# A linear-attention stage: the place of the first units' bias additions, the engine of their copies, and one more unit in written-out order

## The chip, the cores and the metric

The kernel runs on one core of one Trainium2 chip. The metric is the device time of one execution in microseconds (us). A core has five engines with a queue each: TensorE (PE; its weight loads are listed as PEld), VectorE (DVE), ScalarE (ACT), GpSimd (POOL) and SyncE (SP), which issues transfers. Each queue is worked off in its order; engines wait for each other by semaphores.

## The reference

A small vision model: a tokenizer, then two layers, each an attention and a feed-forward block with a residual addition around each. The change lies in the attention of the second layer (the "linear attention"), which is computed so:

```python
def _L1_attn_ref(x, W_qkv, b_qkv, W_out, b_out):
    qkv = x @ W_qkv + b_qkv
    q, k, v = jnp.split(qkv, 3, axis=2)
    q = q - jnp.mean(q, axis=2, keepdims=True)
    k = k - jnp.mean(k, axis=2, keepdims=True)
    q2 = q * q
    k2 = k * k
    q2s = jnp.sum(q2, axis=2, keepdims=True)
    k2s = jnp.sum(k2, axis=2, keepdims=True)
    k2 = _l2_normalize(k2 / (k2s + EPS_DIV), axis=-2)
    q2 = _l2_normalize(q2 / (q2s + EPS_DIV), axis=-1)
    kv = jnp.einsum('bnc,bnd->bcd', k2, v)
    t2 = jnp.einsum('bnc,bcd->bnd', q2, kv) / math.sqrt(N)
    attn = v + t2
    return attn @ W_out + b_out
...
h = h + _L0_ffn_ref(_layernorm(h, axis=-1), ...)
h = h + _L1_attn_ref(_layernorm(h, axis=-1), ...)
h = h + _L1_ffn_ref(_layernorm(h, axis=-1), ...)
```

There are 4 images of 784 distinct rows with 256 columns (each stands three times in the output). `l2_normalize` over axis -2 makes k depend on all rows of an image; q is normalised row by row.

## The kernel before, in words

**Tiles and units.** Rows stand in tiles of 128: six full tiles an image, and one tile (the last) with the 16 rows left over of each image. `h` holds all 25 tiles on chip in f32. The linear attention works in units of three tiles: units 0 to 7 (two an image) and unit LU = 8, the tile of left-over rows.

**What a unit goes through.** `fetch` (GpSimd, L1643) gathers the two expert outputs of each row from memory into `ys`. `stats_one` (VectorE, L1657, L1674, L1675) adds them, weighted, to `h` (two L1657 per tile) and takes mean and variance. `norm_root` (ScalarE, L1687) and `norm_rows` (VectorE, L1696, L1699) make the normalised rows `xa`. `x_t` transposes `xa` on TensorE and copies the result from PSUM to `lxT`; `qk_mm` (TensorE, L1881), `qk_add` (VectorE, L1887) and `qk_squares` (ScalarE, L1895, L1896) make the squares of q and k with their sums; `root` (ScalarE), `factors` (VectorE, L1919 to L1923), `k_rows` (ScalarE, L1928), `q_rows` (VectorE, L1935), `k_squares` (ScalarE, L1942) and `fold` (VectorE, L1956 to L1961) make the normalised k (`uk`), q, and the sum of squares of an image. `q_t` transposes q into `lqT`.

**What an image goes through.** When both its units are ready: `k_x_tiles` multiplies `uk` with `xa` into `pukx` (TensorE, L1980), `k_x_left` adds the left-over rows (L1987), `k_norm` sums the folds over the rows (TensorE into `pn`, L1998 and L1999, then ScalarE L2004 and VectorE L2005), `k_x_out` scales into `g` (VectorE, L2012), `g_t` transposes `g` (TensorE L2028, ScalarE L2031), `kv_out` multiplies with the folded weight Wvo into `pkvo` and `kvo` (L2040, L2044). Then `rows_out(u)` computes, for each tile of a unit, x Wvo + q kvo into `pout` (TensorE, L2055 and L2060) and adds it to `h` (VectorE, L2066).

**Weights and the bias.** `layer1_weights` folds Wv and Wout into Wvo, and the biases into `bvo` and `bres` = bout + bvo (L734 to L753), in three steps taken by `next(steps)`. `residual(u)` (VectorE, L1714) adds `bres` to the three tiles of a unit in `h`. It has to come after the unit's `norm_rows`, which read `h` without it. Before, the first units that are normalised ahead of `bres` are put on the list `pending` and added at unit 3 (L2192); from there on each addition follows its `norm_rows`.

**Copies.** `copy_out` takes turns by a counter: odd to ScalarE (L89), even to VectorE (L91). `bias_relu` uses the same counter, every third to VectorE. The copies of unit LU's lxT go to VectorE without counting.

**What sets the order.** Units 0 to 2 stand in a block under `tc.manual_schedule`, in which the engines run in the order of the text (the scheduler may put instructions from outside the block between them, as it does with additions of L1714). From there on (the loop `for u in range(3, LU + 2)`, L2167) a scheduler sets the order from the dependencies and its own estimate of times. A manual dependency without a semaphore (`NoSync`) tells it only what must come after what on one engine. Seven PSUM buffers named `ps` go round. The last stage, the second feed-forward block with four experts (L2205 on), follows.

## Time and profile before

| | |
|---|---|
| median of 3 runs | 759.25 us (757.95 to 761.08) |
| profiled execution | 760.57 us, of which 758.9 us from the first to the last instruction (the span) |
| mean granted TensorE clock | 0.975 |
| VectorE busy over the span | 480.9 us (63%) |
| ScalarE busy over the span | 331.1 us (44%) |
| first product with Wqkv (unit 0) | 457.0 us |
| last gather issued | 518.0 us |
| loop of the last stage (L2209) | from 616 us to the end |

The profile is of one execution on the chip. Times in it count from the span's start. A group of instructions in order of time is given as start, length, engine, line, operation, tile written and tiles read, shapes and count; in brackets stands how long the engine was idle ahead of it and what ended that. "Clock" is the share of full speed that was granted to TensorE. A duration includes an instruction's start and end, so that independent instructions one behind the other follow at some 0.1 us less.

### The profile page before, as it was taken

How to read it: one execution, taken by the hardware profiler on the slowest of the kernel's cores; microseconds unless marked ns; L12 is line 12 of the kernel's file. 1: busy time of each engine (PE TensorE's matmuls, PEld its weight loads, DVE VectorE, ACT ScalarE, POOL GpSimd, SP SyncE). 2: the span in 40 equal slices, each digit the busy share in tenths (PEclk: the TensorE clock that was granted, in tenths of full speed). 3: DMA queues.
4: the chain of work that ended last, by engine and by line, in shares of the span. 5: the costliest groups of instructions: out<-in, count | busy, mean ns of one | idle time of the engine just before them, and what ended most of it. 6: DMA issues, size and time to landing. Idle time of an engine off the chain costs nothing.

```text
span 758.9 us, 10590 instructions
## 1 busy us (share of the span) xinstructions
PE 698.0 (92%) x3391; PEld 478.9 (63%) x3391; DVE 480.9 (63%) x1521; ACT 331.1 (44%) x782; POOL 127.1 (17%) x231
## 2 busy tenths in 40 slices
PE   6798989999996879998899999888999999999996
PEld 4645565666564568887788874557677765555553
DVE  4666786778999654456544767799957464444441
ACT  0554776555865554342222326353546322222231
POOL 5400000000034607600003036752000000000000
PEclk9999999999999879999999999899999999999998
DMA  8399999100011864422334352321000013222333
GB/s 196 89 426 424 425 424 424 48 1 1 0 36 48 275 239 136 157 83 78 91 98 125 98 161 71 88 79 43 1 0 2 4 29 114 93 76 62 125 108 98
DMA packets 56117, 96.24 MB, mean 127 GB/s; under 512 B 6375, under 2 KB 46030, under 8 KB 56062
## 3 DMA queue, kind: packets, MB, share of 16 engines
q1 hardware_dynamic: 49648, 79.38, 29.6%
q0 software_dynamic: 5536, 14.32, 6.2%
q10 hardware_dynamic: 878, 1.86, 1.0%
q8 instruction: 27, 0.44, 0.2%
q14 instruction: 28, 0.23, 0.1%
HBM read 30.45 MB, written 65.09 MB: 126 GB/s over the span
## 4 chain that ended last, share of the span: by engine, by line
PE 69%; DVE 19%; ACT 5%; DMA 3%; issue 2%; SPq 1%; DVEq 1%; ACTq 0%
PE pb L1420 12%; PE pe L289 6%; PE pyb L1438 5%; PE ps L289 4%; PE pqk L1881 4%; PE pkv L289 4%; PE pt L280 4%; PE pw L558 3%; PE pwp L300 3%; PE ps L2256 3%; PE pout L2055 3%; PE pout L2060 3%; DVE oT L868 2%; PE pukx L1980 2%; DMA img<-in_x_dram 2%
## 5 line engine op out<-in xcount | busy, mean ns | idle before, releaser
L1059 POOL DMA_INDIRECT xrows<-xn,pos x50 | 52.6, 1051 | 238.0 <-DVE nm L918 191.9
L1643 POOL DMA_INDIRECT ys<-yrows,pos x50 | 51.7, 1033 | 142.7 <-DMA yrows<-yb 124.3
L1420 PE MATMUL pb<-xTb,own 128*128 128x256 f32 (+1 forms) x240 | 54.5, 371 | 8.1 <-DVE own L1396 5.4
L1426 ACT ACTIVATE hb<-pb,own 128x256 f32<-128x256 f32 (+1 forms) x74 | 33.8, 456 | 57.8 <-PE pb L1420 51.5
L1420 PE MATMUL pb<-hb,own 128*128 128x256 f32 (+1 forms) x240 | 52.1, 359 | 0.6 <-DVE hb L1428 0.6
L1438 PE MATMUL pyb<-own,hb 128*128 128x256 f32 x216 | 51.8, 381 | 0.2 <-ACT hb L1426 0.2
L1420 PEld LDWEIGHTS pb<-xTb,own 128*128 128x128 f32 x240 | 41.7, 195 | 16.1 <-ACT hb L1426 7.6
L1881 PE MATMUL pqk<-Wqkv,lxT 128*128 128x512 f32 x100 | 46.6, 613 | 0.2 <-ACT lxT L89 0.2
L289 PE MATMUL pe<-xT,eW 128*128 128x512 f32 (+1 forms) x112 | 46.0, 553 | 0.0
L1438 PEld LDWEIGHTS pyb<-own,hb 128*128 128x128 f32 x216 | 40.3, 190 | 5.9 <-ACT hb L1426 0.6
L1420 PEld LDWEIGHTS pb<-hb,own 128*128 128x128 f32 x240 | 40.5, 190 | 5.3 <-DVE hb L1428 1.2
L558 PE MATMUL pw<-Wall,pT 128*128 128x512 f32 x96 | 42.6, 593 | 0.0
L1409 ACT COPY xTb<-ptb 128x512 f32<-128x512 f32 (+1 forms) x30 | 16.2, 540 | 56.4 <-PE ptb L1405 56.4
L1444 DVE TENSOR_TENSOR yb<-pyb,eb 128x512 f32<-128x512 f32 (+1 forms) x30 | 19.1, 638 | 33.9 <-PE pyb L1438 33.5
L280 PE MATMUL pt<-ident,xn 128*128 128x128 f32 x200 | 30.4, 282 | 10.2 <-DVE xn L584 6.6
L280 PEld LDWEIGHTS pt<-ident,xn 128*128 128x128 f32 x200 | 23.5, 142 | 25.2 <-ACT y L561 6.0
L1428 DVE TENSOR_SCALAR hb<-pb,own 128x256 f32<-128x256 f32 (+1 forms) x46 | 20.5, 447 | 27.9 <-PE pb L1420 21.2
L822 DVE SCALAR_TENSOR_TENSOR prod<-kq 128x784 f32<-128x784 f32 x32 | 30.4, 970 | 6.1 <-ACT kq L1236 3.4
L289 PEld LDWEIGHTS pe<-xT,eW 128*128 128x128 f32 x112 | 20.2, 190 | 21.6 <-issue 16.5
L1396 DVE COPY own<-ew 128x1540 f32 x30 | 28.9, 965 | 6.8 <-ACT xTb L1409 2.7
L1895 ACT ACTIVATE qk<-qk 128x256 f32<-128x256 f32 x50 | 20.4, 408 | 28.4 <-DVE qk L1887 26.0
L1881 PEld LDWEIGHTS pqk<-Wqkv,lxT 128*128 128x128 f32 x100 | 19.0, 197 | 20.4 <-issue 17.9
(416 smaller groups left out, 1473.4 us busy)
## 6 DMA issues: line engine op xcount, KB each, us to landing
xrows<-nothing SPq DMA_DIRECT2D x22, 896.0 KB
yrows<-nothing SPq DMA_DIRECT2D x22, 896.0 KB
out_dram<-h SPq DMA_DIRECT2D x23, 384.0 KB
xb<-xrows SPq DMA_DIRECT2D x24, 256.0 KB
yrows<-yb SPq DMA_DIRECT2D x24, 256.0 KB
ew<-in_L_ffn_expert_w_dram SPq DMA_DIRECT2D x6, 768.0 KB
wb<-wd SPq DMA_DIRECT2D x16, 128.0 KB
img<-in_x_dram SPq DMA_DIRECT2D x2, 588.0 KB
```

Source lines behind the costliest of these rows:

```text
L280: nc.tensor.transpose(pt[:, j * TT : (j + 1) * TT], xn[:, j, c * P : (c + 1) * P], ident[:TT, :TT])
L289: nc.tensor.matmul(pm[: wcols.stop - wcols.start, :n], w[:, c, wcols], xT(c), start=(c == 0), stop=(c == chunks - 1),)
L300: nc.tensor.matmul(pm[:, i, :], xT(c, t), w[:, c, :], start=(c == 0), stop=(c == chunks - 1))
L558: nc.tensor.matmul(pm, pixels(c, tiles[j]), Wall[:, c, :], start=(c == 0), stop=(c == 1))
L822: nc.vector.scalar_tensor_tensor(prod, qTs[s][:, o, :], 1.0, kT[:, o, t * SEQ : (t + 1) * SEQ], ALU.mult, ALU.mult, accum_out=atts[s][:, o ...
L1059: put = nc.gpsimd.indirect_dma_start(out=xrows[:, :], out_offset=bass.IndirectOffsetOnAxis(ap=pos[:, k, t0 + j : t0 + j + 1], axis=0), in_ ...
L1396: nc.vector.tensor_copy(w, ewf[0][:, bass.ds(off, EW)])
L1420: nc.tensor.matmul(pm, wm[:, c, o * P : (o + 1) * P], src[:, c, :], start=(c == 0), stop=(c == 1),)
L1426: nc.scalar.activation(dst[:, o, :], pm, AF.Relu, bias=b)
L1438: nc.tensor.matmul(pm[:, t, :], src[:, c, t * P : (t + 1) * P], wm[:, c, :], start=(c == 0), stop=(c == 1),)
L1643: got = nc.gpsimd.indirect_dma_start(out=y[:, j, k, :], out_offset=None, in_=yrows[:, :], in_offset=bass.IndirectOffsetOnAxis(ap=pos[:, k, ...
L1881: nc.tensor.matmul(pqk, xTs[u][:, c, cut(j, 1)], Wqkv[:, c, : 2 * D], start=(c == 0), stop=(c == 1),)
```

## The change

1. A switch `one_side` is on for the written-out block: every `copy_out` in it goes to ScalarE. The copies for `bvs`, `WvT` and `bvo` and those of unit LU's lxT go to ScalarE as well; unit LU's now count in the turn.
2. `residual` is held for the first seven units that are normalised (0, 1, LU, 2, 3, 4, 5). They are added after `rows_out` of units 3 (in the loop at u = 5: units 0 and 1), 4 (u = 6: LU and 2) and 5 (u = 7: 3, 4 and 5), each with an order-only dependency on the last addition of that `rows_out`. Units 6 and 7 are added behind their `norm_rows` as before.
3. In the written-out block, unit 2's statistics and rows move forward, ahead of unit LU's factors and the first folds.
4. The written-out block goes on for one more unit: unit 3, the statistics and rows of unit 4, its transposes and `rows_out` of unit 1 (now a generator, so that its two parts can be placed apart). The loop begins at 4. Statistics of units 5 and later (`behind`) may come no earlier than the end of `rows_out(1)`; before, those of units 4 and later no earlier than the end of `rows_out(0)`.

```diff
@@ copy_out
+    one_side = [False]
...
-        if turn[0] % 2:
+        if one_side[0] or turn[0] % 2:
             nc.scalar.copy(dst, src)
         else:
             nc.vector.tensor_copy(dst, src)
@@ layer1_weights
         for k in range(2):
-            nc.vector.tensor_copy(bvs[:, k, :], col("bv", k).to_broadcast([P, P]))
-        nc.vector.tensor_copy(WvT, pt)
+            nc.scalar.copy(bvs[:, k, :], col("bv", k).to_broadcast([P, P]))
+        nc.scalar.copy(WvT, pt)
...
-        nc.vector.tensor_copy(bvo, pw)
+        nc.scalar.copy(bvo, pw)
@@ norm_rows, residual
-        if pending is None:
+        if len(pending) < 7:
+            pending.append(u)
+        else:
             residual(u)
-        else:
-            pending.append(u)
...
-    def residual(u):
+    def residual(u, last=None):
...
-        nc.vector.tensor_tensor(ht, ht, over(lw[2], n), ALU.add)
+        added = nc.vector.tensor_tensor(ht, ht, over(lw[2], n), ALU.add)
+        if last:
+            tc.add_manual_dep(
+                added.ins, last,
+                mybir.DependencyInfo(mybir.DependencyClass.NoSync, mybir.DependencyReason.DATA),
+                reason="where VectorE has time",
+            )
@@ x_t
-        copy = nc.vector.tensor_copy if u == LU else copy_out
-        transposed(xa_of(u), n, lambda c, pt: copy(xT[:, c, : n * TT], pt))
+        transposed(xa_of(u), n, lambda c, pt: copy_out(xT[:, c, : n * TT], pt))
@@ rows_out
     def rows_out(u):
+        for done in rows_out_parts(u):
+            pass
+        return done
+
+    def rows_out_parts(u):
...
-            done = nc.vector.tensor_tensor(ht, pm[:, : len(two), :], ht, ALU.add)
-        return done
+            yield nc.vector.tensor_tensor(ht, pm[:, : len(two), :], ht, ALU.add)
@@ the written-out block
+    one_side[0] = True
     with tc.manual_schedule(engines=by_hand | {ENG.Pool}):
...
         q_rows(0)
+        stats_one(2, 0)
         next(steps)
         x_t(LU)
         q_t(0)
         k_rows(0)
         next(steps)
-        stats_one(2, 0)
+        stats_one(2, 1)
         factors(1)
         q_rows(1)
         k_rows(1)
         qk_mm(LU, 0)
+        stats_one(2, 2)
+        norm_root(2)
         next(steps)
         Wvo, bvo = lw[:2]
         q_t(1)
         qk_add(LU, 0)
         qk_squares(LU, 0)
         root(LU)
-        stats_one(2, 1)
-        stats_one(2, 2)
+        norm_rows(2)
         fetch(5)
-        norm_root(2)
         squares[0] = k_squares(0)
         factors(LU)
         fold(0, squares.pop(0))
-        norm_rows(2)
         k_rows(LU)
...
-        behind.append(rows_out(0).ins.name)
+        rows_out(0)
         x_t(3)
-    squares[2] = scales(2)
-    fold(2, squares.pop(2))
-    for u in range(3, LU + 2):
+        root(2)
+        factors(2)
+        k_rows(2)
+        q_rows(2)
+        fetch(6)
+        for j in range(2):
+            qk_mm(3, j)
+            qk_add(3, j)
+            qk_squares(3, j)
+            stats_one(4, j)
+        squares[2] = k_squares(2)
+        qk_mm(3, 2)
+        qk_add(3, 2)
+        qk_squares(3, 2)
+        stats_one(4, 2)
+        root(3)
+        norm_root(4)
+        norm_rows(4)
+        parts_ = rows_out_parts(1)
+        next(parts_)
+        fold(2, squares.pop(2))
+        factors(3)
+        k_rows(3)
+        q_t(2)
+        x_t(4)
+        for done in parts_:
+            pass
+        q_rows(3)
+        squares[3] = k_squares(3)
+        fold(3, squares.pop(3))
+        behind.append(done.ins.name)
+    one_side[0] = False
+    later = {5: (0, 1), 6: (2, 3), 7: (4, 5, 6)}
+    for u in range(4, LU + 2):
...
-        if u == 3:
-            for k in pending:
-                residual(k)
-            pending = None
-        rows_out(u - 2)
+        done = rows_out(u - 2)
+        for k in later.get(u, ()):
+            residual(pending[k], done.ins.name)
```

`later` holds places in the list `pending`, whose order is 0, 1, LU, 2, 3, 4, 5.

## The prediction

> **What bounds the kernel now.** Read in this order: the page's first part, the chain of waits, the engines in order of time through the first units of the linear attention, and the granted clock in 2 us windows. Page, part one:
>
> ```profile
> PE 698.0 (92%) x3391; PEld 478.9 (63%) x3391; DVE 480.9 (63%) x1521; ACT 331.1 (44%) x782; POOL 127.1 (17%) x231
> ```
>
> TensorE is busy for 92% of the span. A new order can only win in the other 8% and in stretches at a lower clock. The chain of waits from 519 us to the end (start, length, what):
>
> ```profile
> 531.15 3.44 PE pqk L1881 x8
> ...
> 601.41 0.59 ACT gT L2031
> ```
>
> From 519.84 us the chain is TensorE almost throughout, with one break of 0.6 us at 601.4 (a ScalarE copy) until the last additions at 752. 531.15 is the start of unit 4's product with Wqkv; from there 221 us of TensorE work follow without a gap worth naming. What moves this start moves the end by as much, if VectorE and ScalarE keep up. Before it the chain runs over VectorE. TensorE in order of time, with the idle time ahead of each group and its releaser in brackets:
>
> ```profile
> 470.86 1.99 PE L741 MATMUL pwvo<-Wout,WvT 128*128 128x256 f32 x8 [0.54 <-DVE WvT L735]
> ...
> 484.06 1.30 PE L280 MATMUL pt<-ident,xa 128*128 128x128 f32 x6 [2.64 <-DVE xa L1699]
> ...
> 505.37 5.48 PE L1881 MATMUL pqk<-Wqkv,lxT 128*128 128x512 f32 x12 [0.24 <-ACT lxT L89]
> 514.77 1.22 PE L280 MATMUL pt<-ident,xa 128*128 128x128 f32 x6 [3.93 <-DVE xa L1699]
> ```
>
> With 0.83 at 497.30 (pkvo, for ScalarE's gT) these are all its waits from 470 to 545. The two large ones are for `xa`, the normalised rows of units 2 and 4 (L1699). The windows (length, then busy us of PE, PEld, DVE, ACT and POOL, the granted clock, the DMA share and GB/s):
>
> ```profile
> 482.00:484.00 2.00, 0.00 (x0) 0.00 (x0) 1.41 (x6) 1.97 (x7) 1.39 (x2) 1.00 0.28 74
> ...
> 486.00:488.00 2.00, 2.00 (x8) 1.30 (x6) 1.35 (x4) 0.00 (x0) 1.70 (x2) 0.50 0.05 10
> ...
> 512.00:514.00 2.00, 0.00 (x0) 0.00 (x0) 2.00 (x9) 1.68 (x8) 1.41 (x2) 1.00 0.23 66
> ...
> 516.00:518.00 2.00, 2.00 (x6) 1.57 (x6) 2.00 (x6) 2.00 (x7) 1.39 (x3) 0.50 0.36 119
> ```
>
> After each large wait TensorE runs at clock 0.50. By 0.2 us windows the half clock lasts from 485.3 to 492.1 and from 516.0 to 519.4: 6.8 and 3.4 us. In these TensorE has no idle time, so the loss is half: 3.4 + 1.7 = 5.1 us. Why VectorE is late with unit 2's rows is seen in its own order of time:
>
> ```profile
> 469.67 0.61 DVE L734 COPY bvs<-cols 128x128 f32<-128x128 f32 x1
> 470.13 0.68 DVE L735 COPY WvT<-pwv 128x512 f32<-128x512 f32 x1
> ...
> 477.73 0.95 DVE L1714 TENSOR_TENSOR h<-h,bout 128x768 f32<-128x768 f32 x1
> ...
> 483.59 1.06 DVE L1699 TENSOR_SCALAR xa<-h,mv,rstd 128x256 f32<-128x256 f32 x3
> ```
>
> Between the q rows of unit 0 (end 469.6) and unit 2's `xa` stand copies (bvs, WvT, two for unit LU, two lqT, bvo), bias additions (L1714: 0.95, and 0.42 at 479.00) and unit LU's factors with a fold that waits for ScalarE. For unit 4 the chain of waits shows:
>
> ```profile
> 513.44 0.86 DVE h L1657 x2
> 514.30 0.34 DVE xa L1699
> ```
>
> Two L1657 that belong to unit 5 are pulled ahead of unit 4's rows; a bias addition (0.84 at 510.73) stands before them.
>
> [...] (6.8 and 3.4 us are two windows and one; the two onsets lie 30.7 us apart, nine windows) [...] waits of 2.64 and 3.93 us sufficed, with TensorE busy in about 1.2 us of the window before the fall. [...] here the two L1657 at 471.59 took 1.56 us beside GpSimd's L2104 (470.25 to 473.95) and 0.99 elsewhere, so +0.57. [...] the trace has 0.48 and 0.55 (L89, L91), so the moved copies get no dearer.
>
> **The change, part by part.** The program's order is known for every engine: up to the q rows of unit 0 only one copy (second half of unit 1's lxT) differs; GpSimd's and SP's orders don't differ at all, so all gathers stand where they stood.
>
> (a) Copies to ScalarE. Up to unit 2's rows VectorE loses bvs and WvT and the lxT of LU and lqT of unit 0 (469.61 to 471.67: 2.06 us) and bvo and one lqT (0.43 + 0.46). ScalarE gets them in its queue: after root(1) at 470.4 come two bvs (not shown on ScalarE; between 0.24, its 128-column copy, and 0.37, its 256-column one; less 0.1 of overlap each: about 0.4 for both, ends 0.3 to 0.55) and WvT (0.58 as gT L2031), so WvT is ready at 471.35 and not 470.75. TensorE's wait of 0.54 grows by 0.55. Nothing hides that: cost 0.55.
>
> (b) Bias additions. L1714 of units 0, LU, 2 and later are gone from 477.7 on; seven are held and put after rows_out of units 3, 4 and 5. VectorE in order, from 469.61: statistics of unit 2, three times 1.6 us (two L1657, L1674, L1675), two of them +0.57; factors(1) 0.72; q rows 0.91: at 477.2. Then it waits for ScalarE (rstd 0.3, bvo 0.37) and does bout (0.42), the qk addition of LU (0.60), reciprocal and three `xa` rows (0.35 each): rows ready from 479.5 to 480.2, not from 484.0. The gathers they need were issued at latest at 469.28, land in 2.7 us, and are asked for at 475.6: hidden.
>
> (c) TensorE from 471.35: pwvo 1.72, pqk of LU 1.72, pbvo 0.87, lqT 0.66, pukx 5.35: 481.7 to 482.0. Unit 2's transposes find their rows. Their lxT copies, both on ScalarE now, stand behind all k squares. ScalarE: squares of LU from 478.9, root, k squares of unit 0 to 481.4, LU's row, then four squares (483.1), two lxT copies (484.0). TensorE is at its pn at 483.6 and asks for lxT at 484.25: met by 0.25 us, so a delay above that comes through. The wait of 2.64 and the cold 6.8 us go. The next wait, for gT (0.83), stays, since it hangs on the same three ScalarE squares. pkvo starts at 490.9 where the trace has 497.30: 6.4 us gained (2.64 + 3.4 + 0.6 of row-by-row waiting in the transposes, less 0.55, and 0.3 of pipeline ends).
>
> (d) Order carried on. pkvo 1.73, pout of unit 0 5.17, transposes 0.65, wait 0.3, so unit 3's pqk at 498.8 to 503.9; two tiles of pout of unit 1 (3.45) and lqT of unit 2 (0.66) now stand ahead of unit 4's transposes: 508.05. VectorE meanwhile: factors(2) at 500.0 (root(2) stands behind two lxT copies on ScalarE), q rows 0.9, then three times a qk addition (0.60) and statistics of unit 4 (1.6): 507.5; rstd 0.3, reciprocal, rows from 508.5 to 509.2. TensorE waits some 0.65 in all, where it waited 3.93 and then had 3.4 us cold. Last tile of pout 1.72, pukx, pn and the left part 6.9, lqT of unit 3 0.66: unit 4's pqk at 518.6, not 531.15. That is 6.1 more (3.3 of wait, 1.7 of cold clock, 0.6 row by row, 0.5 pipeline ends), 12.5 so far.
>
> What ScalarE queues here: k rows of unit 3 wait for factors(3) at about 511, and lqT of unit 2 and lxT of unit 4 stand behind them, ready at 514. TensorE asks for lxT(4) at 518.6: hidden, 4 us to spare. The fold's last addition is at about 516, as pn comes up: 0 to 0.5.
>
> (e) Later units. The late bias additions, 0.87 each, are on VectorE's queue: two of them stand ahead of the last fold addition of unit 5, for which pn of image 2 waits: between 0 (fold done in time) and 1.7; I take 1.0. The added dependency only orders, it brings no semaphore wait. The other five stand beside gate and softmax work, under TensorE's 5 us pqk groups. VectorE's load bears it: from 470 to 620 it is busy 113.6 us, of which some 6.3 us are copies now on ScalarE; 107 us remain for about 138. In the last stage ReLUs change engine (unit LU's copies now count in the turn: both of e1 go to ScalarE, s2 and one s1 to VectorE), each needed 2 us or more after it is ready: 0, or up to 0.2 in each of seven groups, 1.4 in all.
>
> Sum: 12.5 - 1.0 = 11.5 us. The profiled execution took 760.57 (span 758.9), so 749.1; its own span would be 747.4. It lies 1.32 above the median of 759.25, about what one cold window more or less is worth (1.7), and so the gain against the median is 10.2.
>
> **Rivals.**
> 1. Smaller gain, a new cold window. TensorE waits at 470.3 for 1.05 us, after 1 us of small waits since 467.9; by the trace a window with 1.2 us busy fell, one with 1.76 (509.1 to 512.5) did not. Here some 1.1 to 1.3 are busy in the window that would end at 471.65. For: that. [...] Cost 1.7 to 3.4; with 0.5 for thin lxT margins and 0.4 more at the end, 752 to 754, say 753.
> 2. Off the path but given back: VectorE has fewer statistics done ahead (the trace has the last L1657 of all units at 536.2), so units 5 to 7 meet them inside TensorE's time. If each of the two rows of units 5 and 6, two pn and two g waits costs 1.2, 7.2 are lost: 756.3, no change. Against: VectorE needs about 14.0 of TensorE's 16.2 us per unit (qk additions 1.8, factors 0.5, q rows 0.9, fold 1.05, rows_out 0.95, copies 0.95, half an image's kn, g and kvo 1.0, statistics 4.8, rows 1.15, bias 0.9).
> 3. Slower. The one mechanism: VectorE falls behind in units 4 to 7, because its strict queue holds held additions ahead of folds and g; TensorE then waits at pn of images 1 to 3, and each wait over 2.6 us brings a half clock of 3.4 us more. Three waits of 3.5 plus three times 1.7 is 15.6: 764.7. It decides only if VectorE's 14.0 us per unit become 21. Against: from 498 to 546 VectorE was busy nearly throughout, and after 520 TensorE didn't wait.
> 4. The change doesn't do what it says: excluded by the order, in which the additions do stand late.
>
> **How the numbers follow.** Forecast 0.73, rival 1 0.17, rival 2 0.06, rival 3 0.04. The forecast's own range is 746.5 to 751.5 (no loss in (e) to 1.7 + 1.4, and 1 us of scatter); with most of rival 1 the range is 746 to 753.5. What a measurement can tell here is about 0.5%, 3.8 us: faster is below 755.45. Forecast and rival 1 are faster, rival 2 the same, rival 3 slower: 0.90, 0.06, 0.04.
>
> **What would show it.** Right: no TensorE wait above 1.2 us between 470 and 530 and clock 1.00 there; pkvo at about 491, unit 4's pqk at about 518.6; no L1714 ahead of that pqk (the trace of before has six by 516). Wrong: clock 0.50 after 471.65 (rival 1); waits for VectorE at pn L1998 or pkvo after 520 (rivals 2 and 3); a wait for lxT from ScalarE near 484 would show that the moved copies became the bound. If the two cold stretches were the accident of this one execution, the gain against the median shrinks by up to 3 us.

## The result, and the profile after

| | kernel before | changed kernel |
|---|---|---|
| median of the runs | 760.16 us (757.95 to 762.25) | 750.86 us (750.06 to 751.87) |
| profiled execution: time | 760.57 us | 750.06 us |
| profiled execution: span, granted clock | 758.9 us, 0.975 | 748.2 us, 0.982 |

The ratio after to before is 0.9876, with a 95% interval of 0.9848 to 0.9905: 9.3 us of the medians and 10.5 us between the two profiled executions. The first part of the changed kernel's page:

```profile
PE 692.6 (93%) x3391; PEld 476.9 (64%) x3391; DVE 475.4 (64%) x1506; ACT 333.1 (45%) x795; POOL 125.4 (17%) x231
```

TensorE's busy time is 5.4 us less (698.0 before) for the same 3391 products. That is for the most part half clock that is gone (5.1 us by the prediction's count). The rest of the 10.7 us of span is idle time that is gone. Which waits they were is seen in TensorE's order of time (start, length, line, operation, and in brackets the idle time ahead and its releaser), the same view that the prediction shows of the kernel before:

```profile
471.37 1.99 PE L742 MATMUL pwvo<-Wout,WvT 128*128 128x256 f32 x8 [1.00 <-ACT WvT L736]
...
481.65 0.82 PE L281 MATMUL pt<-ident,xa 128*128 128x128 f32 x6
...
483.64 0.38 PE L2004 MATMUL pn<-ones,acc 128*128 128x1 f32 x2 [0.29 <-DVE acc L1967]
...
491.70 1.99 PE L2046 MATMUL pkvo<-Wvo,gT 128*128 128x256 f32 x8 [1.10 <-ACT gT L2037]
...
499.77 5.42 PE L1887 MATMUL pqk<-Wqkv,lxT 128*128 128x512 f32 x12 [0.24 <-ACT lxT L90]
...
509.55 1.21 PE L281 MATMUL pt<-ident,xa 128*128 128x128 f32 x6 [0.25 <-DVE xa L1700]
```

Of the two large waits for `xa`, the one of 2.64 us is gone (481.65 carries no bracket) and the one of 3.93 us has become 0.25. Two other waits have grown: for WvT from 0.54 to 1.00 and for gT from 0.83 to 1.10. A small one is new, 0.29 for the fold at pn. The windows (busy us of PE, PEld, DVE, ACT and POOL, granted clock, DMA share, GB/s):

```profile
482.00:484.00 2.00, 1.71 (x13) 1.25 (x11) 1.27 (x4) 1.42 (x5) 1.50 (x2) 1.00 0.25 66
486.00:488.00 2.00, 2.00 (x6) 0.83 (x5) 1.97 (x5) 0.62 (x3) 1.54 (x2) 1.00 0.37 98
512.00:514.00 2.00, 2.00 (x11) 1.76 (x10) 1.48 (x5) 2.00 (x6) 1.70 (x2) 1.00 0.46 131
516.00:518.00 2.00, 2.00 (x14) 1.67 (x13) 1.90 (x7) 0.00 (x0) 0.00 (x0) 1.00 0.22 66
```

At 486 and 516 us the clock column reads 1.00 where it read 0.50; no stretch between 446 and 548 us is at half clock. VectorE in order of time shows why the rows are early:

```profile
469.57 1.09 DVE L1658 SCALAR_TENSOR_TENSOR h<-ys,wk,h 128x256 f32<-128x256 f32 x2
...
471.26 1.25 DVE L1658 SCALAR_TENSOR_TENSOR h<-ys,wk,h 128x256 f32<-128x256 f32 x2
...
477.30 0.42 DVE L754 TENSOR_TENSOR bout<-bout,bvo 128x256 f32<-128x256 f32 x1 [0.62 <-ACT bvo L752]
477.64 0.68 DVE L1893 TENSOR_TENSOR qk<-pqk,bqkv 128x512 f32<-128x512 f32 x1
...
478.44 1.06 DVE L1700 TENSOR_SCALAR xa<-h,mv,rstd 128x256 f32<-128x256 f32 x3
...
508.99 1.06 DVE L1700 TENSOR_SCALAR xa<-h,mv,rstd 128x256 f32<-128x256 f32 x3
...
531.40 0.95 DVE L1715 TENSOR_TENSOR h<-h,bout 128x768 f32<-128x768 f32 x1
```

The rows of unit 2 (L1700, 478.44) come behind bout's addition and one qk addition, 5.2 us earlier than before. No bias addition (L1715) stands ahead of them or of unit 4's rows at 508.99; the first is at 531.40. The chain of waits of the changed kernel from 518.9 us on (start, length, what):

```profile
518.91 0.65 PE pukx L1993 x3
519.56 0.66 PE pt L281 x6
520.22 3.44 PE pqk L1887 x8
```

Unit 4's product starts at 520.22, where it was 531.15: 10.93 us gained, of which 10.67 remain at the end of the chain. The later units gave back about 0.3.

### The profile page after: what moved, and what is told of

It reads as the page before. It is cut to its first block, busy times and chain, and to the rows that moved or that the text cites. A ratio compares the mean times of both kernels' runs of the same rounds, so it can differ in the third digit from the quotient of the medians.

```text
span 748.2 us, 10591 instructions
## 1 busy us (share of the span) xinstructions
PE 692.6 (93%) x3391; PEld 476.9 (64%) x3391; DVE 475.4 (64%) x1506; ACT 333.1 (45%) x795; POOL 125.4 (17%) x231
## 4 chain that ended last, share of the span: by engine, by line
PE 69%; DVE 18%; ACT 7%; DMA 2%; issue 2%; DVEq 1%; ACTq 0%
PE pb L1421 12%; PE pe L290 6%; PE pyb L1439 5%; PE ps L290 4%; PE pqk L1887 4%; PE pkv L290 4%; PE pt L281 3%; PE pw L559 3%; PE ps L2296 3%; PE pwp L301 3%; PE pout L2066 3%; PE pout L2071 3%; DMA img<-in_x_dram 2%; DVE oT L869 2%; PE pukx L1986 2%
## 5 line engine op out<-in xcount | busy, mean ns | idle before, releaser
L1644 POOL DMA_INDIRECT ys<-yrows,pos x50 | 49.2, 983 | 141.2 <-DMA yrows<-yb 124.4
L1887 PE MATMUL pqk<-Wqkv,lxT 128*128 128x512 f32 x100 | 44.9, 594 | 0.2 <-ACT lxT L90 0.2
L1439 PEld LDWEIGHTS pyb<-own,hb 128*128 128x128 f32 x216 | 40.3, 190 | 5.8 <-ACT hb L1427 0.6
L281 PE MATMUL pt<-ident,xn 128*128 128x128 f32 x200 | 29.9, 278 | 10.7 <-DVE xn L585 6.6
L559 PEld LDWEIGHTS pw<-Wall,pT 128*128 128x128 f32 x96 | 18.0, 190 | 19.9 <-issue 17.7
L1887 PEld LDWEIGHTS pqk<-Wqkv,lxT 128*128 128x128 f32 x100 | 18.4, 190 | 19.3 <-issue 17.0
```

What stands on the lines that cost most here:

```text
L281: nc.tensor.transpose(pt[:, j * TT : (j + 1) * TT], xn[:, j, c * P : (c + 1) * P], ident[:TT, :TT])
L559: nc.tensor.matmul(pm, pixels(c, tiles[j]), Wall[:, c, :], start=(c == 0), stop=(c == 1))
L1439: nc.tensor.matmul(pm[:, t, :], src[:, c, t * P : (t + 1) * P], wm[:, c, :], start=(c == 0), stop=(c == 1),)
L1644: got = nc.gpsimd.indirect_dma_start(out=y[:, j, k, :], out_offset=None, in_=yrows[:, :], in_offset=bass.IndirectOffsetOnAxis(ap=pos[:, k, ...
L1887: nc.tensor.matmul(pqk, xTs[u][:, c, cut(j, 1)], Wqkv[:, c, : 2 * D], start=(c == 0), stop=(c == 1),)
```

## The experiments

The ratios stand against runs of the kernel before on the same chip. Executions also differ by up to 3 us in the first 457 us, which no kernel here changes (the first product with Wqkv, unit 0's, starts between 456.5 and 459.4 in the fourteen profiles; the recorded expectations call it unit 1's). So each profile is also read from that product on, and the time column is used to see whether the reading holds. The columns: median of the runs and ratio with interval; then, from unit 0's product, the us to pkvo of image 0 and to unit 4's product; from unit 0's product to the last output transfer that ScalarE issues; and the half clock between 460 and 540 us, in us.

| kernel | median | ratio | pkvo | unit 4 | end | half clock |
|---|---|---|---|---|---|---|
| before | 760.16 | | 40.3 | 74.0 | 295.9 | 10.2 |
| changed | 750.86 | 0.9876 [0.9848, 0.9905] | 34.7 | 63.0 | 285.2 | 0 |
| bias_early | 752.09 | 0.9892 [0.9873, 0.9911] | 35.7 | 64.5 | 286.7 | 3.4 |
| copies_back | 752.72 | 0.9900 [0.9883, 0.9916] | 38.0 | 66.4 | 288.6 | 6.8 |
| block_short | 751.72 | 0.9887 [0.9869, 0.9906] | 34.7 | 64.1 | 286.0 | 0 |
| bias_alone | 755.67 | 0.9947 [0.9930, 0.9964] | 36.3 | 69.1 | 291.0 | 3.4 |
| stats_back | 753.14 | 0.9915 [0.9896, 0.9934] | 36.6 | 64.9 | 287.0 | 0 |
| bias_inblock | 752.72 | 0.9909 [0.9890, 0.9928] | 36.6 | 65.8 | 287.7 | 3.4 |
| warm | 758.80 | 0.9981 [0.9970, 0.9993] | 37.7 | 71.3 | 293.1 | 3.4 |
| copies_stats | 759.59 | 1.0001 [0.9987, 1.0015] | 36.2 | 70.4 | 293.2 | 10.2 |
| after_again | 749.57 | 0.9872 [0.9847, 0.9898] | 34.7 | 63.1 | 285.2 | 0 |
| after_warm | 751.26 | 0.9896 [0.9870, 0.9921] | 34.9 | 63.2 | 285.4 | 0 |
| better | 750.13 | 0.9880 [0.9860, 0.9899] | 33.4 | 61.7 | 283.8 | 0 |
| better_again | 750.24 | 0.9885 [0.9859, 0.9911] | 33.6 | 61.8 | 284.0 | 0 |

The starts are those of TensorE in order of time, where unit 4's product of the changed kernel stands at 520.05. From unit 4's product to the end all fourteen take 221.8 to 222.8 us: everything is decided between 457 and 531 us.

Each profile is of one execution. Two profiles of the same kernel agree to 0.2 us in these columns (changed and after_again, better and better_again). The times are coarser: by their intervals bias_early, copies_back, block_short, stats_back and bias_inblock can't be told from the changed kernel, and only bias_alone, warm and copies_stats stand clear of it. What the five are said to cost is read from their profiles.

**bias_early: the additions let go as before, all at the loop's first turn (now u = 4), the rest of the change kept.**

```diff
-        if len(pending) < 7:
-            pending.append(u)
-        else:
+        if pending is None:
             residual(u)
...
-        done = rows_out(u - 2)
-        for k in later.get(u, ()):
-            residual(pending[k], done.ins.name)
+        if u == 4:
+            for k in pending:
+                residual(k)
+            pending = None
+        rows_out(u - 2)
```

> The changed kernel with its bias additions of the first units back where the kernel before let them go: all held ones together after rows_out of unit 2's turn (u == 4), later ones right behind the rows of their own unit; no order tie. Copies on ScalarE, unit 2's statistics early and the order carried on through unit 4's rows stay. Theory A (the time came from getting unit 2's and unit 4's rows out earlier, by whatever means, and the hold list already keeps the additions behind unit 4's rows here, because the release now comes after the written-out block): unit 4's pqk (L1887) still starts at 520 +-1 us, time about 750.5, within 1 us of the changed kernel. Theory B (the later placement of the additions is what brings the gain; the order around them only follows): three to five additions of 0.87 us stand in VectorE's way again, folds and gates of units 2 to 5 come late, waits of TensorE return after 520 us: 754 to 758.

Measured: 752.09, ratio 0.9892; unit 4's product 64.5 us after unit 0's, where the changed kernel needs 63.0. VectorE in order of time, additions (L1715) and rows (L1700) of units 2 to 4:

```profile
479.55 0.40 DVE L1715 TENSOR_TENSOR h<-h,bout 128x256 f32<-128x256 f32 x1
479.87 1.05 DVE L1700 TENSOR_SCALAR xa<-h,mv,rstd 128x256 f32<-128x256 f32 x3
...
480.96 0.96 DVE L1715 TENSOR_TENSOR h<-h,bout 128x768 f32<-128x768 f32 x1
...
499.45 0.95 DVE L1715 TENSOR_TENSOR h<-h,bout 128x768 f32<-128x768 f32 x1
...
500.86 0.96 DVE L1715 TENSOR_TENSOR h<-h,bout 128x768 f32<-128x768 f32 x1
...
510.47 1.06 DVE L1700 TENSOR_SCALAR xa<-h,mv,rstd 128x256 f32<-128x256 f32 x3
```

The additions are back among the rows: 0.40 us stand ahead of unit 2's, and 1.9 us (499.45, 500.86) ahead of unit 4's. Yet the wait for unit 4's rows is 0.24 us. Most of the 1.5 us have another source, which TensorE and the windows of this kernel show:

```profile
471.82 3.26 PE L742 MATMUL pwvo<-Wout,WvT 128*128 128x256 f32 x8 [1.00 <-ACT WvT L736]
```

```profile
472.00:474.00 2.00, 2.00 (x6) 1.59 (x7) 1.90 (x5) 2.00 (x7) 2.00 (x3) 0.60 0.00 0
474.00:476.00 2.00, 2.00 (x5) 1.23 (x4) 1.78 (x8) 1.21 (x5) 1.79 (x2) 0.55 0.00 0
```

Behind the same wait of 1.00 us that the changed kernel has, 3.4 us at half clock follow here: pkvo comes 1.0 us later. Half of 3.4 would be 1.7; 0.3 of the wait at pn and 0.1 of that for gT were taken up, and 0.3 stays unexplained. The other 0.5 us arise between pkvo and unit 4's product. So theory A in the main, with a half clock on top, but not as it was put: it had the additions behind unit 4's rows, and they stand ahead of them. By this profile the late additions are worth some 0.5 us when the rest of the change is in place. And the prediction's first rival, a half clock after the wait for WvT, is real; the profiled execution of the changed kernel was spared it.

**copies_back: bvs, WvT, bvo and unit LU's lxT copied by VectorE again, and the switch `one_side` off,** so that the other copies of the written-out block take turns as before.

```diff
-            nc.scalar.copy(bvs[:, k, :], col("bv", k).to_broadcast([P, P]))
-        nc.scalar.copy(WvT, pt)
+            nc.vector.tensor_copy(bvs[:, k, :], col("bv", k).to_broadcast([P, P]))
+        nc.vector.tensor_copy(WvT, pt)
...
-        nc.scalar.copy(bvo, pw)
+        nc.vector.tensor_copy(bvo, pw)
...
-        transposed(xa_of(u), n, lambda c, pt: copy_out(xT[:, c, : n * TT], pt))
+        copy = nc.vector.tensor_copy if u == LU else copy_out
+        transposed(xa_of(u), n, lambda c, pt: copy(xT[:, c, : n * TT], pt))
...
-    one_side[0] = True
```

> The changed kernel with the copies of bvs, WvT, bvo and unit LU's lxT on VectorE again (as in the kernel before) and nothing else undone. Theory A (the copies are 2 to 3 us of VectorE's work just ahead of unit 2's rows, part of its lateness there): VectorE now does three statistics of unit 2 ahead of them or between, WvT is late, TensorE waits 2 to 2.5 us at pwvo instead of 1.0, and some 1.8 us are lost: 752.5; if this wait brings the half clock on, 1.7 to 3.4 more, 754 to 756. Theory B (the copies were hidden anyway, only the additions mattered): 750.5 +-0.7, wait at pwvo not above 1.2.

Measured: 752.72. The wait at pwvo and the windows behind it:

```profile
471.81 3.78 PE L742 MATMUL pwvo<-Wout,WvT 128*128 128x256 f32 x8 [1.91 <-DVE WvT L736]
```

```profile
470.00:472.00 2.00, 0.18 (x1) 0.19 (x2) 1.93 (x8) 1.55 (x4) 2.00 (x3) 0.80 0.23 66
472.00:474.00 2.00, 2.00 (x5) 1.64 (x6) 1.93 (x5) 0.07 (x1) 1.86 (x2) 0.50 0.00 0
474.00:476.00 2.00, 2.00 (x5) 1.37 (x5) 1.79 (x9) 0.67 (x3) 1.68 (x2) 0.50 0.13 29
476.00:478.00 2.00, 2.00 (x4) 0.72 (x3) 1.32 (x4) 1.50 (x5) 1.39 (x3) 0.50 0.32 102
```

The wait is 1.91 us, since WvT now stands in VectorE's queue behind unit 2's statistics, and two windows at half clock follow (471.2 to 478.0). From unit 0's product to unit 4's it is 3.3 us longer in this profile, where 0.9 of wait and 3.4 of half clock would make 4.3; of the difference 0.6 was taken from the wait for gT (0.83 instead of 1.10) and the fold's (0.29, gone). Theory A: the wait came, a little under the 2 to 2.5 us expected, and the half clock with it, but the median is the one expected without a half clock. Which of the two groups of copies costs how much stays open, since no run parts them.

**block_short: the written-out order ends with unit 2, as before.**

```diff
-        rows_out(0)
+        behind.append(rows_out(0).ins.name)
         x_t(3)
-        root(2)
-        factors(2)
...
-        behind.append(done.ins.name)
+    squares[2] = scales(2)
+    fold(2, squares.pop(2))
...
-    for u in range(4, LU + 2):
+    for u in range(3, LU + 2):
```

> The changed kernel with the written-out order ending where it ended before (the plain loop starts at u = 3 instead of 4), the copies, the early statistics of unit 2 and the late additions kept. Theory A (unit 4's rows come out in time once no bias addition and no copy stands in front of them; the longer written-out order adds little): transposes of unit 4 wait about 2 us for xa instead of 0.25, but one of the things that stand behind them moves ahead, so unit 4's pqk starts at 520 to 521: 750.5 to 751.5; if the wait of 2 us brings the half clock, 752.5 to 754. Theory C (the second half of the gain, 4 to 6 us, is the longer written-out order): wait for xa(4) of 3.5 us or more with clock 0.50 after it, unit 4's pqk at 524 or later: 754.5 to 757.

Measured: 751.72; TensorE at unit 4's transposes:

```profile
509.33 0.41 PE L281 MATMUL pt<-ident,xa 128*128 128x128 f32 x2 [1.78 <-DVE xa L1700]
```

The wait for unit 4's rows is 1.78 us instead of 0.25, without a half clock, and unit 4's product is 1.1 us later. Theory A; the second half of the gain is not the longer order's, as long as the additions stay late.

**copies_stats: copies and early statistics alone.** The kernel of block_short, with the additions let go as in the kernel before.

```diff
-        if len(pending) < 7:
-            pending.append(u)
-        else:
+        if pending is None:
             residual(u)
...
-        done = rows_out(u - 2)
-        for k in later.get(u, ()):
-            residual(pending[k], done.ins.name)
+        if u == 3:
+            for k in pending:
+                residual(k)
+            pending = None
+        rows_out(u - 2)
```

> The first and the third part of the change without the other two: copies on ScalarE and unit 2's statistics early, but additions and written-out order as in the kernel before. With the longer order kept and the additions early the time was that of the changed kernel, and with the late additions kept and the short order nearly so (1 us). Theory A (late additions and longer order stand in for each other: either alone gets unit 4's rows out in time): without both, pkvo of image 0 still starts some 34 to 35 us after unit 1's pqk, as in the changed kernel, but the wait for xa(4) of 3.5 to 4.5 us returns with a half clock behind it, and the time is 754.5 to 757. Theory E (neither counts for unit 4's rows once copies are gone and statistics are early): wait for xa(4) not above 2 us, 751 to 752.5.

Measured: 759.59, no change against before (14 runs, 758.13 to 761.15). The mechanism of theory A came, its time did not:

```profile
510.48 1.74 PE L281 MATMUL pt<-ident,xa 128*128 128x128 f32 x6 [3.66 <-DVE xa L1700]
```

```profile
510.00:512.00 2.00, 1.52 (x6) 1.26 (x7) 2.00 (x9) 0.82 (x3) 1.56 (x2) 0.50 0.48 131
512.00:514.00 2.00, 2.00 (x7) 1.64 (x6) 1.99 (x5) 1.77 (x6) 1.52 (x2) 0.50 0.41 94
514.00:516.00 2.00, 2.00 (x6) 1.55 (x6) 2.00 (x8) 0.00 (x0) 0.50 (x1) 0.50 0.36 111
```

The wait for unit 4's rows is back at 3.66 us with two windows at half clock around it (509.3 to 516.2), and there is one more behind the wait at pwvo. The profiled execution was the fastest of the fourteen, which goes some way to explain why its column is 2.7 us below before while the median isn't. What follows, by the profiles: early additions cost 1.5 us with the long order (bias_early, where the plain loop lets them go one turn later), 1.0 of it from a half clock behind a wait that the changed kernel has too; the short order costs 1 us with late additions (block_short); both together cost 8 us (10 by the medians on one chip, against after_again). That is far more than the sum: for unit 4's rows the two parts stand in for each other.

**bias_alone: the late additions alone, in the kernel before.** The edit is the counterpart of bias_early's, with `later = {5: (0, 1), 6: (2, 3), 7: (4, 5, 6)}` and the tie behind rows_out.

> The kernel before with the late bias additions alone (seven held, released behind rows_out of units 3, 4 and 5, with the order tie); copies, statistics of unit 2 and the written-out order as before. Theory A (lateness of two rows, made by additions, copies and order together): the wait for unit 2's xa falls from 2.64 to about 1.8 us and with it perhaps its half clock; the wait for unit 4's xa stays near 3.8 with a half clock behind it: 3 to 6 us faster than before, 754 to 757. Theory B (the additions alone bring it): both waits go, 750 to 752. Theory D (the additions bring nothing by themselves): 759 to 760, both waits and both half clocks as before.

Measured: 755.67, as theory A had it. Both waits for `xa` remain:

```profile
482.72 1.30 PE L280 MATMUL pt<-ident,xa 128*128 128x128 f32 x6 [1.74 <-DVE xa L1699]
...
509.82 0.57 PE L280 MATMUL pt<-ident,xa 128*128 128x128 f32 x2 [3.51 <-DVE xa L1699]
```

At 1.74 us the first has no half clock behind it any more (clock 1.00 from 482 to 490); the second, 3.51 us, still has one, of 3.4 us. So late additions alone give 4 to 5 of the 10 us.

**stats_back: unit 2's statistics, root and rows at their old places.**

```diff
         q_rows(0)
-        stats_one(2, 0)
         next(steps)
...
-        stats_one(2, 1)
+        stats_one(2, 0)
         factors(1)
...
         qk_mm(LU, 0)
-        stats_one(2, 2)
-        norm_root(2)
         next(steps)
...
         root(LU)
-        norm_rows(2)
+        stats_one(2, 1)
+        stats_one(2, 2)
         fetch(5)
+        norm_root(2)
...
         fold(0, squares.pop(0))
+        norm_rows(2)
         k_rows(LU)
```

> The changed kernel with unit 2's statistics, root and rows back at their old places in the written-out order (one place later each); copies on ScalarE, late additions and the longer order stay. Theory A (unit 2's rows must be out before TensorE has done unit LU's products, and each thing put ahead of them on VectorE delays them): rows of unit 2 come about 1.3 to 2 us later, TensorE waits 1.0 to 1.5 us for xa(2) where the changed kernel waits nothing, pkvo and all after it about 1.5 to 2 us later: 752 to 753 (1.7 more if a half clock follows). Theory E (with additions and copies gone VectorE has slack there, the earlier statistics are not needed): 750.5 to 751.5, no wait for xa(2).

Measured: 753.14; unit 2's transposes wait again:

```profile
483.80 1.37 PE L281 MATMUL pt<-ident,xa 128*128 128x128 f32 x6 [1.27 <-DVE xa L1700]
```

1.27 us of wait, pkvo and unit 4's product 1.9 us later: theory A, in the place and of the size expected (the median lies 0.1 above its range).

**bias_inblock: the additions inside the written-out order, where the kernel before had them.**

```diff
         root(LU)
+        residual(0)
+        residual(LU)
         norm_rows(2)
...
         fold(0, squares.pop(0))
+        residual(2)
...
         x_t(3)
+        residual(1)
...
         qk_squares(3, 2)
+        residual(3)
         stats_one(4, 2)
...
-    later = {5: (0, 1), 6: (2, 3), 7: (4, 5, 6)}
+    later = {7: (5, 6)}
```

> The changed kernel with its bias additions at the places inside the written-out order where the kernel before had them on VectorE: units 0 and LU ahead of unit 2's rows, 2 behind them, 1 behind unit 2's transposes, 3 ahead of unit 4's last statistics; two are left for later. Copies on ScalarE, early statistics and longer order stay. Theory A (the parts overlap: with copies gone and statistics early some 1.4 us of additions ahead of unit 2's rows nearly fit, and one of 0.9 ahead of unit 4's rows shows as 1 us of wait): 1 to 2 us slower than the changed kernel, 751.5 to 752.5 (1.7 more if a half clock follows). Theory B (the additions are the cause of both waits): wait for xa(2) of 2 us or more and for xa(4) of 3 us or more return, with half clocks, 755 to 758.

Measured: 752.72. TensorE:

```profile
471.45 3.67 PE L742 MATMUL pwvo<-Wout,WvT 128*128 128x256 f32 x8 [1.00 <-ACT WvT L736]
...
485.60 0.38 PE L2004 MATMUL pn<-ones,acc 128*128 128x1 f32 x2 [0.48 <-DVE acc L1967]
...
512.27 1.21 PE L281 MATMUL pt<-ident,xa 128*128 128x128 f32 x6 [1.11 <-DVE xa L1700]
```

and VectorE, the additions (L1715):

```profile
479.10 1.28 DVE L1715 TENSOR_TENSOR h<-h,bout 128x768 f32<-128x768 f32 x2
...
508.60 0.95 DVE L1715 TENSOR_TENSOR h<-h,bout 128x768 f32<-128x768 f32 x1
```

Unit 2's rows are in time although 1.28 us of additions (479.10) stand ahead of them, but the fold behind them is later: pn waits 0.48 us, where bias_early has no wait, and pkvo comes 0.9 us later than there. With 0.95 us (508.60) ahead of unit 4's last statistics, unit 4's transposes wait 1.11 us instead of 0.25. Behind the wait of 1.00 us at pwvo there was a half clock of 3.4 us in this execution. Theory A again; theory B's waits of 2 and 3 us did not come.

**warm: products that nothing reads, in the wait for unit 2's rows, in the kernel before.** Nothing is left out of the computation; five products are added.

```diff
         k_x_tiles(0)
+        warm = ps_tile("warm")
+        for _ in range(5):
+            nc.tensor.matmul(warm[:, :D], ident, Wout[:, 0, :], start=True, stop=True)
         x_t(2)
```

> The kernel before, with five products of 128x256 added that nothing reads (ident with Wout into a spare PSUM buffer), issued ahead of unit 2's transposes, so that TensorE is busy during most of its wait for xa(2) (some 1.1 us at full clock, right behind the last k_x product). The wait itself stays. It parts the two terms of the first gain of 6.4 us, the wait (2.64) and the half clock after it (3.4). If the half clock is on the path and follows from TensorE's idle time: clock 1.00 from 484 to 492, pkvo 2.5 to 3.4 us earlier than 497.3, time 756 to 757.5. If TensorE at half clock only ate slack that the waits for VectorE and ScalarE would have taken anyway: clock 1.00, but pkvo within 1 us of 497.3, time 759 to 760. If the clock falls all the same: nothing changes but the extra products, 760.

Measured: 758.80 (22 runs), ratio 0.9981 [0.9970, 0.9993]: 1.4 us faster, more work notwithstanding, but short of the 756 to 757.5 expected if the half clock is on the path. TensorE and the windows:

```profile
481.96 2.32 PE L2145 MATMUL warm<-Wout,ident 128*128 128x256 f32 x10
484.87 1.30 PE L280 MATMUL pt<-ident,xa 128*128 128x128 f32 x6 [0.59 <-DVE xa L1699]
...
487.84 0.38 PE L1998 MATMUL pn<-ones,acc 128*128 128x1 f32 x2 [0.80 <-DVE acc L1961]
...
495.64 1.99 PE L2040 MATMUL pkvo<-Wvo,gT 128*128 128x256 f32 x8 [0.83 <-ACT gT L2031]
```

```profile
484.00:486.00 2.00, 1.41 (x8) 0.76 (x7) 1.96 (x8) 1.45 (x5) 1.65 (x2) 1.00 0.42 123
486.00:488.00 2.00, 1.21 (x8) 0.74 (x6) 1.90 (x5) 0.36 (x1) 1.74 (x1) 1.00 0.21 66
488.00:490.00 2.00, 2.00 (x11) 1.41 (x12) 0.89 (x4) 0.26 (x1) 1.39 (x3) 1.00 0.24 66
```

The added products took 2.3 us, twice what was expected, and covered most of the wait. The rows are no earlier, but the clock stays at 1.00 from 482 to 490, where the kernel before has 0.50. pkvo comes 2.6 us earlier in this profile, not 3.4: a wait for the fold of 0.80 us, which the half clock had covered, shows instead. By this profile the half clock is on the path and follows from TensorE's idle time: clock and pkvo moved as that theory said. The median moved by about half of what the profile says; why, no run shows.

**after_again and after_warm.** The changed kernel once more, and with four such products ahead of pwvo.

```diff
         q_t(0)
+        warm = ps_tile("warm")
+        for _ in range(4):
+            nc.tensor.matmul(warm[:, :D], ident, Wout[:, 0, :], start=True, stop=True)
         k_rows(0)
```

> The changed kernel itself, on the chip of the next two, as their measure. Its profile had a wait of 1.00 us at pwvo and no half clock behind it; the kernel with the early additions had the same wait and half clock for 3.4 us. If that half clock falls on some executions only, by where the clock's windows stand: times of two kinds about 1.7 us apart, 749 to 753, median 750.5 to 751.5. If it never comes in this kernel: all within 1 us.

> The changed kernel with four products of 128x256 added that nothing reads, ahead of pwvo, so that TensorE is busy in most of its 1.0 us wait for WvT. If that wait brings on the half clock in some executions (1.7 us each): clock 1.00 from 470 to 550, times 0.5 to 1.5 us below the changed kernel's of the same chip and closer together. If the half clock seen there in other kernels has another cause, or the added products push pwvo back: within 0.5 us of it.

Measured: 749.57 (749.23 to 751.82) and 751.26 (750.23 to 751.73). The run of 751.82 is the profiled one; it has no half clock between 460 and 745 us, and its unit 0 product simply started 1.8 us later than in the first profile, so this one slow time doesn't come from pwvo. The times don't all lie within 1 us, and the one that stands apart isn't slow by a half clock, so neither theory of after_again is shown. The warmed kernel has no wait at pwvo and clock 1.00, but its products pushed pwvo back by 0.7 us, of which 0.2 reach unit 4's product, and its median is 1.7 above after_again's: no gain, and by the profile no such loss. How often the changed kernel meets the half clock at pwvo stays open: over the seven profiles with that wait of 1.00 us (both of the changed kernel, bias_early, block_short, stats_back, bias_inblock, copies_stats) three have it.

**better: the two waits that were left.** ScalarE copies WvT ahead of unit 1's last q squares and of bvs, and image 0's gate with gT goes ahead of unit 2's second q squares and of lqT of LU.

```diff
+        nc.scalar.copy(WvT, pt)
+        yield
         bvs = w1p.tile([P, 2, P], F32, tag="bvs", name="bvs")
...
-        nc.scalar.copy(WvT, pt)
-        yield
...
         qk_add(1, 2)
+        next(steps)
         qk_squares(1, 2)
...
         stats_one(2, 0)
-        next(steps)
         x_t(LU)
...
         qk_add(2, 1)
+        gT = g_t(0)
         qk_squares(2, 1)
         q_t(LU)
-        gT = g_t(0)
```

> The changed kernel with two moves of ScalarE's order: WvT's copy ahead of unit 1's third q squares and of the two bvs copies, and image 0's gate with the copy of gT ahead of the q squares of unit 2's second tile and of lqT of LU. If the two waits that the changed kernel keeps (1.00 us for WvT at 470.4, 1.10 us for gT at 490.6) are ScalarE's order alone: the first falls to about 0.6, the second below 0.4, unit 4's pqk 1.0 to 1.6 us earlier, 749 to 749.8, and with the first wait shorter fewer executions with a half clock behind it. If another thing is right behind (VectorE's gate, the transposes' lqT, unit 3's lxT): pqk of unit 3 and 4 where they were, 750.5 to 751.5.

> The kernel with WvT's copy and image 0's gate moved ahead on ScalarE again, beside the changed kernel on one chip. Its trace gave 1.4 us between unit 1's pqk and unit 4's pqk (61.7 against 63.0) and no half clock there. If this holds for most executions: 1 to 2 us below the changed kernel of this call. If its gain was that one execution's: within 0.5 us.

```profile
471.32 1.89 PE L742 MATMUL pwvo<-Wout,WvT 128*128 128x256 f32 x8
...
484.75 0.38 PE L2004 MATMUL pn<-ones,acc 128*128 128x1 f32 x2 [1.07 <-DVE acc L1967]
...
491.56 1.89 PE L2046 MATMUL pkvo<-Wvo,gT 128*128 128x256 f32 x8
```

Both waits are gone. TensorE now comes to pn 1 us sooner, but the fold doesn't, so the first gain is given back there (1.07 us at 484.75, where the changed kernel waits 0.29); pn starts 26.6 us after unit 0's product in both. What remains is the wait for gT: unit 4's product comes 1.2 to 1.4 us earlier in both profiles, as expected. The medians (750.13, 750.24) don't differ from the changed kernel's (750.86, 749.57) and miss the 749 to 749.8 expected, so a gain of this size isn't shown by the times.

## Why the prediction was right, and where its terms were off

The forecast was 749.1 us for the profiled execution; it took 750.06. The gain there was 10.5 us instead of 11.5, and the mechanism was the one named: rows of units 2 and 4 early, both large waits and both half clocks gone. By its steps:

- (a) TensorE's wait for WvT. pwvo was expected from 471.35 and came at 471.37, with a wait of 1.00.
- (b) Unit 2's rows were expected from 479.5 and came from 478.86 to 479.5 (the three L1700 end one after another). The pairs of L1658 beside GpSimd were priced at +0.57 each and took 1.09 and 1.25 us, which is +0.10 and +0.26.
- (c) Transposes of unit 2 without a wait, as written. pkvo was put at 490.9 and came at 491.70. The missing 0.8 is a wait for gT of 1.10 that had been left at 0.83, a wait of 0.29 for the fold at pn, which wasn't expected, and some 0.2 that no wait accounts for. The half clock had been booked at 3.4 us in this step; warm shows 2.6, because part of it had covered the fold.
- (d) Unit 4's product at 518.6; it came at 520.22 in the chain, 10.93 us gained and not 12.5. Of the 1.6 missing, half comes from (c); the rest was added between pkvo and unit 4's product, in small pieces. The mechanism held: a wait of 0.25 for unit 4's rows, clock 1.00.
- (e) A loss of 1.0 in the later units was charged; it was 0.26. The fold of image 2 was almost in time.
- The sum, then, was 0.8 us above the 10.67 at the end of the chain because a gain put 1.6 us too high met a loss put 0.7 too high. That the two errors offset each other is luck.

Two things that the total doesn't show. First, the parts were priced as a chain in which each edit brings its own share. They are not additive: alone, late additions give 4 to 5 us and copies with early statistics nothing in the median; taken from the whole, each part costs 0.9 to 3.4 us by the profile, half clocks included. What counts is when two sets of rows leave VectorE, and more than one edit gets them out. Second, the rival of a half clock behind the wait for WvT got a chance of 0.17. So low a figure was the author's estimate, and the trace of before did not support it: the clock fell there behind windows with 1.2 us busy, and some 1.1 to 1.3 were expected here. In three of seven profiles with this wait the half clock came, so the rival was underrated. Its working also put the window's end at 471.65, which fits the trace of before (485.27 less four windows of 3.41), but the windows' places differ between executions: in the profiled one of the changed kernel they end at 469.36 and 472.77. That both profiled executions of the changed kernel were spared is luck, and of the others it isn't known.

Rivals 2 and 3 (VectorE gives the time back in units 5 to 7) fell: after unit 4's product the changed kernel needs 222.1 us to the end, the kernel before 221.9.

## What to carry to other kernels

When the bound engine waits for rows from another one, count each wait and any half clock behind it (in the kernel before, 6.8 us behind a wait of 2.64 and 3.4 behind one of 3.93), and ask when the rows leave: several edits can get them out. Here, with copies and statistics in place, late additions or the longer order alone came within 0.9 to 1.5 us of having both, and without either 8 us were lost. Test an edit by taking it from the finished kernel and by putting it alone on the old one; the two answers differ when parts stand in for each other. Where executions scatter by more than the effect, measure from an event ahead of the change to one behind it within each profile.

## What the runs showed of the hardware

The granted clock changes on a grid of 3.41 us (a window is one step of it), and where its windows stand matters. In the kernel before, it changes from 480 us on at 485.27, 492.10, 515.99, 519.40 and 754.92 us: the later four lie 2, 9, 10 and 79 times 3.4133 us behind the first. In the traces of before and of the changed kernel all falls of the clock (eight and seven) lie on one such grid each to within 0.01 us. For the other twelve a grid agrees with the clock in windows of 10 us to about 0.1 us. Its place differs between executions.

By this grid TensorE was busy for 0.1 to 1.2 us of the window ahead of five of the falls between 460 and 540 us, but for 1.5 us in copies_back and 1.8 in bias_early, bias_inblock and copies_stats. No window with more was followed by a fall. Three windows with 1.7 to 1.8 us passed without one (before from 509.2, block_short from 505.9, bias_alone from 479.2), so busy time alone doesn't decide in this range. In the four falls 1.2 to 1.6 us of the busy time were transposes (products with `ident`), in the three that passed none was. No run varies this alone.

The grid also parts the three profiles of seven in which the same waits ahead of pwvo brought a half clock from the other four. In these three a window began 2.8 to 3.3 us ahead of pwvo and held both the wait of 1.00 us and one of 0.6 before it. In the other four a window began 1.9 to 2.1 us ahead, so that the two waits lay in two windows, busy for 2.4 and 2.6 us. In the changed kernel's trace a window is busy for at most 1.82 us if it begins 2.8 to 3.6 us ahead of pwvo, about a quarter of all places. So if all places were alike, one execution in four would have the half clock there: an estimate. after_warm, better and better_again have no stretch of 3.4 us between 460 and 540 with less than 2.3 us busy, and no fall there.

The falls between 460 and 540 us last 3.4 or 6.8 us, as in the kernel before, and nothing between.

VectorE's pairs of L1658 beside GpSimd's work took 0.10 to 0.57 us more (1.09, 1.25 and 1.56 against 0.99; no run sets GpSimd apart as the cause), so one such reading is a poor price for the next.

VectorE kept the order of its queue where that cost time: in the changed kernel it was idle for 0.62 us ahead of bout's addition (477.30, for ScalarE's bvo), while the product that the qk addition behind it (L1893, 477.64) reads had ended at 475.08 (L1887, from 473.20).
